# A triangle product in four channels at a time: three of four channels of the core with seventeen half-width products, in place of two of three

## The chip, the cores and the metric

The kernel runs on one core of a Trainium2 chip. The metric is the device time of one execution in microseconds (us). Before the change the median of three runs is 3130.55 us (3130.3 to 3131.14).

## The reference, cut to what matters

The input is x, 384 x 384 positions with 128 features. Two layers follow each other. The first holds the operation that this change is about:

```python
z = _layernorm(x, norm_g, norm_b)
left = (z @ Wl + bl) * jax.nn.sigmoid(z @ Wlg + blg)
right = (z @ Wr + br) * jax.nn.sigmoid(z @ Wrg + brg)
core = jnp.einsum('bikh,bjkh->bijh', left, right)
zo = _layernorm(core, onorm_g, onorm_b) @ Wout + bout
```

The einsum is, for each of the 128 channels h, a product of two 384 x 384 matrices. The core is then normalized over the channels, so the kernel also keeps for every position (i, j) the sum over the channels and the sum of squares. The second layer (a gated product with row sums) is not touched.

## The kernel before, in words

The kernel has three stages in time. The first normalizes x, makes left and right and writes them to a scratch tensor lr_d in HBM. The second is the core: channel by channel it loads left and right of the channel (the tile lrh, both interleaved), multiplies, and writes the result ct to core_d. The third reads core_d back and does everything else. Each wrapped instruction (`seq`) keeps its place in the program, so on every engine the order is the order of the code.

The change is in the second stage, in the loop over h at line 671. A channel's matrices are cut in blocks of 128 rows; N is 384 and J, half the width, 192. A product of one 128 x 128 block with 192 columns is called a half product here. There are two ways to do a channel:

- **Kind 0** (lines 675 to 695) is the plain way: nine products of 384 columns, eighteen half products, into three PSUM banks full3.
- **Kinds 1 and 2** (lines 696 to 747) compute the upper left 2 x 2 corner with seven products in place of eight, in the manner of Strassen and Winograd. They do three products of 384 columns into the bank b4 (third block row), and eleven half products into four banks b0 to b3: seventeen half products. GpSimd prepares sums of left blocks (`left_sums`, 613, four additions) and of right halves (`right_sums2`, 622, three subtractions) into small buffers, two sets of them (`sss`, `tts`). VectorE combines the banks: base and three terms (731 to 734), then `join` (661), which adds b0 and b1 to their terms and writes the first block row of ct, and `close` (665), which does this for b2 and b3, stores the channel and adds it to csum.

Before the change the kind is h % 3, for h from 0 to 125: 42 channels of each kind. The last two channels are done apart, plainly (754 on).

What stands in which place matters here. Everything that prepares channel h + 1 is issued inside channel h: `stay` (608, two copies of kept data on GpSimd), `left_sums`, `right_sums2` (if h + 1 is of kind 1 or 2), and `apart` (632), three ScalarE copies that take right out of the interleaved tile. The squares are made by `squares` on ScalarE (636) and added by `add_squares` on VectorE (639, 384 columns). At the end of a channel of kind 1 VectorE does one `add_squares` and then `join(h)` (743, 744); the next channel, of kind 2, starts with `close(h - 1)`. At the end of a channel of kind 2 VectorE does two `add_squares` (746, 747); `join` and `close` come only in the next channel, of kind 0, after its products were issued (679 to 681). All matmuls of these channels are issued by `product` at line 649; the VectorE additions out of PSUM by `add` at line 652.

A kind 0 channel uses the banks full3, so it does not touch b0 to b3, from which `join` and `close` still read. A channel of kind 1 or 2 starts with a product into b0 (699), then three into b4 (701), then b1, b2, b3 (728 to 730).

Loads of lrh (`load_h`, 85, called at 749) run three channels ahead, on SyncE's queue, as do the stores of ct.

Of the kernel before, what the change touches and what calls it, by code (L numbers as in the profile page):

```python
# [19 lines left out]
def triangle_then_gated_row_kernel(ctx: ExitStack, tc: tile.TileContext, a: dict, out: bass.AP):  # L20
# [17 lines left out]
    H = a["L0_side_b"].shape[0] // 4  # L38
# [17 lines left out]
    def seq(ins):  # L56

        return tc.keep_in_program_order(ins)
# [21 lines left out]
    with ExitStack() as ctx2:  # L80
# [481 lines left out]
        with tc.tile_pool(name="p2r", bufs=2, side="right", reuse_waits="tile") as rrp, \  # L562
# [9 lines left out]
            right = {}  # L572

            def fill(h):

                if h < H:
# [15 lines left out]
                    if h == 0:  # L592
                        stay()

            J = N // 2
            js = slice(0, J), slice(J, N)
            terms2 = arena[:, 2:4].rearrange("p b n -> p (b n)").rearrange("p (q j) -> p q j", j=J)
            base = arena[:, 6, js[0]]
            tts = [arena[:, n:n + 2].rearrange("p b n -> p (b n)").rearrange("p (q j) -> p q j", j=J) for n in (0, 4)]
            sss = [[arena[:, 2 * NB + 1, n * P:(n + 1) * P] for n in range(3)] + [arena[:, 6, J:J + P]],  # L600
                   [wz[:, n * P:(n + 1) * P] for n in range(4)]]
            sq = arena[:, NB:2 * NB]
            cts = {}
# [8 lines left out]

            def left_sums(h):

                ss = sss[h % 3 - 1]
                for n, x, y, op in ((0, block(h, 0, 1), block(h, 0, 0), ALU.subtract),
                                    (1, block(h, 0, 1), block(h, 1, 1), ALU.add),
                                    (2, ss[1], block(h, 0, 0), ALU.subtract),
                                    (3, block(h, 1, 0), ss[2], ALU.subtract)):
                    seq(nc.gpsimd.tensor_tensor(ss[n], x, y, op))  # L620

            def right_sums2(h):

                rr, tt = right[h], tts[h % 3 - 1]
                seq(nc.gpsimd.tensor_tensor(
                    tt[:, 0:2], rr[:, 0, js[1]].unsqueeze(1).to_broadcast([P, 2, J]),
                    rr.rearrange("p b n -> p (b n)").rearrange("p (a m) -> p a m", a=2)[:, :, js[0]], ALU.subtract,
                ))
                seq(nc.gpsimd.tensor_tensor(tt[:, 2], rr[:, 0, js[0]], tt[:, 1], ALU.subtract))
                seq(nc.gpsimd.tensor_tensor(tt[:, 3], rr[:, 1, js[0]], tt[:, 2], ALU.subtract))  # L630

            def apart(h, k):

                seq(nc.scalar.copy(right[h][:, k], loaded2[h][:, k, :, 1]))  # L634
# [4 lines left out]
            def add_squares(c, ib=slice(0, NB)):  # L639
                seq(nc.vector.tensor_add(csq[:, ib], c, csq[:, ib]))  # L640
# [14 lines left out]
            with tc.tile_pool(name="p2mix", bufs=1, space=PSUM, reuse_waits="tile") as mps:  # L655
                full3 = [mps.tile([P, 512], F32, name="r%d" % n)[:, :N] for n in range(NB)]
                half4 = [mps.tile([P, 512], F32, name="b%d" % n) for n in range(4)]
                b4 = mps.tile([P, 512], F32, name="b4")[:, :N]
                b0, b1, b2, b3 = (b[:, :J] for b in half4)

                def join(h):
                    for b, j, n in (b0, js[0], 0), (b1, js[1], 1):
                        add(cts[h][:, 0, j], b, terms2[:, n])

                def close(h):
                    for b, j, n in (b2, js[0], 2), (b3, js[1], 3):
                        add(cts[h][:, 1, j], b, terms2[:, n])
                    store_core(h)
                    add_sum(cts[h])

                for h in range(H - 2):
                    cts[h] = op.tile([P, NB, N], F32, tag="ct", name="ct")
                    right[h + 1] = rrp.tile([P, NB, N], F32, tag="rr", name="rr")
                    kind, rr, ct = h % 3, right[h], cts[h]
                    if kind == 0:
                        for i in range(NB):
                            for k in range(NB):
                                product(full3[i], block(h, k, i), rr[:, k], k == 0, k == NB - 1)
                        if h > 0:
                            join(h - 1)  # L680
                            close(h - 1)
                        stay(h + 1)
                        left_sums(h + 1)
                        for k in range(NB - 1):
                            apart(h + 1, k)
                        right_sums2(h + 1)
                        seq(nc.scalar.copy(ct[:, 0], full3[0]))
                        if h > 0:
                            for ib in range(NB):
                                squares(cts[h - 1][:, ib], half4[ib][:, :N])  # L690
                                add_squares(half4[ib][:, :N], ib)
                        apart(h + 1, NB - 1)
                        seq(nc.scalar.copy(ct[:, 1], full3[1]))
                        for ib in range(2):
                            add_sum(full3[ib], ib)
                    else:
                        ss, tt = sss[kind - 1], tts[kind - 1]
                        B = [[rr[:, k, j] for j in js] for k in range(NB)]
                        product(b0, block(h, 0, 0), B[0][0])
                        for k in range(NB):  # L700
                            product(b4, block(h, k, 2), rr[:, k], k == 0, k == NB - 1)
                        stay(h + 1)
                        if kind == 1:
                            seq(nc.scalar.copy(cts[h - 1][:, 2], full3[2]))
                            store_core(h - 1)
                            add_sum(full3[2], 2)
                            seq(nc.scalar.copy(terms2[:, 0], b0))
                            left_sums(h + 1)
                            for ib in range(2):
                                squares(full3[ib], full3[ib])  # L710
                                add_squares(full3[ib], ib)
                            for k in range(NB - 1):
                                apart(h + 1, k)
                            right_sums2(h + 1)
                            seq(nc.scalar.copy(ct[:, 2], b4))
                            squares(full3[2], full3[2])
                        else:
                            close(h - 1)
                            seq(nc.scalar.copy(terms2[:, 0], b0))
                            for ib in 0, 2:  # L720
                                squares(cts[h - 1][:, ib], full3[ib])
                            apart(h + 1, 0)
                            squares(cts[h - 1][:, 1], full3[1])
                            apart(h + 1, 1)
                            add_squares(full3[0], 0)
                            seq(nc.scalar.copy(ct[:, 2], b4))
                        apart(h + 1, NB - 1)
                        product(b1, ss[2], tt[:, 2])
                        product(b2, ss[1], tt[:, 0])
                        product(b3, ss[0], tt[:, 1])  # L730
                        add(base, b1, terms2[:, 0])
                        add(terms2[:, 2], b3, base)
                        add(terms2[:, 1], b2, base)
                        add(terms2[:, 3], b3, terms2[:, 1])
                        product(b0, block(h, 1, 0), B[1][0], True, False)
                        product(b0, block(h, 2, 0), B[2][0], False, True)
                        product(b1, ss[3], B[1][1], True, False)
                        product(b1, block(h, 2, 0), B[2][1], False, True)
                        product(b2, block(h, 1, 1), tt[:, 3], True, False)
                        product(b2, block(h, 2, 1), B[2][0], False, True)  # L740
                        product(b3, block(h, 2, 1), B[2][1])
                        if kind == 1:
                            add_squares(full3[2], 2)
                            join(h)
                        else:
                            for ib in 1, 2:
                                add_squares(full3[ib], ib)
                    del right[h], loaded2[h]
                    load_h(h + 3)
                join(h)  # L750
                close(h)
            with tc.tile_pool(name="p2ps", bufs=2, space=PSUM, reuse_waits="tile") as ps, \
                 tc.tile_pool(name="p2one", bufs=1, space=PSUM, reuse_waits="tile") as ps1:
                for h in range(H - 2, H):
                    t, rr = loaded2.pop(h), right.pop(h)
# [16 lines left out]
                    ct = op.tile([P, NB, N], F32, tag="ct", name="ct")  # L772
# [363 lines left out]
```

## Time and profile before

The profiled execution took 3133.74 us by its own time; its span from the first to the last instruction is 3131.9 us, so 1.8 us lie around it. It is 3.2 us (0.1%) above the median of the three runs.

| | first stage | core, h < 126 | last two channels | third stage |
|---|---|---|---|---|
| stretch of the span, us | 0 to 1011 | 1011 to 1719 | 1719 to 1740 | 1740 to 3132 |
| TensorE busy, us | 1005.6 | 706.9 | 20.2 | 1378.7 |
| VectorE busy, us | 833.7 | 566.7 | 13.7 | 1226.3 |
| ScalarE busy, us | 491.5 | 439.1 | 12.9 | 1014.3 |
| GpSimd busy, us | 813.9 | 450.7 | 5.8 | 1117.2 |
| share of the DMA engines | 0.77 | 0.98 | 0.94 | 0.61 |

How to read it and the lines below: PE is TensorE's matmul, PEld its weight load, DVE is VectorE, ACT ScalarE, POOL GpSimd, SP SyncE. Busy time counts only stretches in which an instruction of the engine was running; the end of a matmul is modelled, so consecutive matmuls overlap in the records, and the pace is read from their starts. A float32 matmul of the program is executed as two passes, and each pass is one record. A row of the timeline is: start, length, engine, line, operation, out<-in, shape, count, and in brackets the idle time of the engine before it and what ended it.

### The profile page before, as it was taken

How to read it: one execution, taken by the hardware profiler on the slowest of the kernel's cores; microseconds unless marked ns; L12 is line 12 of the kernel's file. 1: busy time of each engine (PE TensorE's matmuls, PEld its weight loads, DVE VectorE, ACT ScalarE, POOL GpSimd, SP SyncE). 2: the span in 40 equal slices, each digit the busy share in tenths (PEclk: the TensorE clock that was granted, in tenths of full speed). 3: DMA queues.
4: the chain of work that ended last, by engine and by line, in shares of the span. 5: the costliest groups of instructions: out<-in, count | busy, mean ns of one | idle time of the engine just before them, and what ended most of it. 6: DMA issues, size and time to landing. Idle time of an engine off the chain costs nothing.

```text
span 3131.9 us, 48235 instructions
## 1 busy us (share of the span) xinstructions
PE 3111.3 (99%) x12146; PEld 2234.8 (71%) x12146; DVE 2640.4 (84%) x8415; ACT 1957.8 (63%) x4551; POOL 2387.5 (76%) x3150
## 2 busy tenths in 40 slices
PE   9999999999999999999999999999999999999998
PEld 4677777777776777777777666777777777777776
DVE  8888888888886778877878788888888888888998
ACT  4444444444444666665665577777777777777776
POOL 6888888888886666666666588788887888888887
PEclk9999999999999999999999999999999999999999
DMA  4888878788783999999999866666666666666562
GB/s 154 330 310 295 336 273 332 288 320 314 289 336 91 283 293 293 293 294 292 293 294 294 281 217 224 217 221 217 221 222 222 222 222 215 222 218 221 204 217 107
DMA packets 509124, 797.66 MB, mean 255 GB/s; under 512 B 56689, under 2 KB 419569, under 8 KB 492466
## 3 DMA queue, kind: packets, MB, share of 16 engines
q1 hardware_dynamic: 507952, 793.20, 74.5%
q8 instruction: 101, 1.65, 0.2%
q14 instruction: 173, 1.42, 0.1%
q10 hardware_dynamic: 834, 1.18, 0.1%
q0 software_dynamic: 64, 0.20, 0.0%
HBM read 508.14 MB, written 286.36 MB: 254 GB/s over the span
## 4 chain that ended last, share of the span: by engine, by line
PE 98%; DVE 1%; issue 0%; POOL 0%; ACT 0%; DMA 0%; POOLq 0%; ACTq 0%; DVEq 0%; SPq 0%
PE pr L372 31%; PE b L649 15%; PE py L934 8%; PE pr L905 8%; PE pg L922 8%; PE pl L923 8%; PE r L649 8%; PE pg L874 8%; PE py L935 4%; DMA core_d<-ct 0%; PE pc L764 0%; POOL rs L286 0%; PE pq L882 0%; PE pt L335 0%; DVE lr L385 0%
## 5 line engine op out<-in xcount | busy, mean ns | idle before, releaser
L372 PE MATMUL pr<-wz,xc 128*128 128x512 f32 x2176 | 935.2, 592 | 1.4 <-POOL xc L324 1.4
L372 PEld LDWEIGHTS pr<-wz,xc 128*128 128x128 f32 x2176 | 670.5, 308 | 265.4 <-POOL xc L324 2.8
L383 ACT ACTIVATE sg<-pr,rs 128x256 f32<-128x256 f32 x1152 | 482.7, 470 | 510.9 <-ACT sg L383 355.4
L385 DVE SCALAR_TENSOR_TENSOR lr<-pr,rs,sg 128x256 f32<-128x256 f32 x1152 | 501.9, 477 | 165.5 <-ACT sg L383 160.1
L969 ACT ACTIVATE py<-py,nm,rs 128x128 f32<-128x128 f32 x1149 | 492.1, 429 | 158.4 <-DVE u L927 80.9
L934 PEld LDWEIGHTS py<-wo,u 128*128 128x128 f32 x2304 | 376.6, 191 | 97.5
L934 PE MATMUL py<-wo,u 128*128 128x128 f32 x2304 | 402.1, 275 | 0.0
L896 POOL TENSOR_TENSOR cs<-ct,rt 128x384 f32<-128x384 f32 x380 | 378.5, 997 | 10.2 <-DMA rt<-rstd_d 6.7
L1004 POOL TENSOR_TENSOR yt<-yt,lnb 128x384 f32<-128x384 f32 x380 | 379.6, 1000 | 2.9 <-DVE yt L998 2.6
L649 PE MATMUL b<-rr,lrh 128*128 128x192 f32 (+1 forms) x1512 | 374.4, 379 | 0.0
L324 POOL TENSOR_TENSOR xc<-xc,bc 128x512 f32<-128x512 f32 x272 | 345.7, 1271 | 24.0
L286 POOL TENSOR_TENSOR rs<-nd,mhalf 128x8 f32<-128x8 f32 (+1 forms) x145 | 236.2, 1629 | 147.0 <-ACT sg L383 107.4
L949 DVE BATCH_NORM_STATS2 st<-py 128x6 f32<-128x128 f32 x1152 | 266.5, 287 | 88.1 <-PE py L935 86.1
L905 PE MATMUL pr<-cs,wc 128*128 128x384 f32 x768 | 313.6, 490 | 1.4 <-DVE cs L894 1.4
L935 PE MATMUL py<-ident,x1T 128*128 128x128 f32 x1152 | 314.0, 273 | 0.0
L922 PE MATMUL pg<-x1T,mat_L_conv_W_gate 128*128 128x384 f32 x768 | 310.7, 486 | 0.9 <-ACT g L925 0.9
L874 PE MATMUL pg<-xt,mat_L_conv_Wg 128*128 128x384 f32 x768 | 310.7, 487 | 0.2 <-ACT ct L788 0.2
L923 PE MATMUL pl<-x1T,mat_L_conv_W_left 128*128 128x384 f32 x768 | 310.5, 486 | 0.0
L649 PEld LDWEIGHTS b<-rr,lrh 128*128 128x128 f32 x1512 | 268.4, 196 | 53.0
L634 ACT COPY rr<-lrh 128x384 f32<-128x384 f32 x378 | 204.7, 549 | 149.4 <-DMA lrh<-lr_d 89.8
L925 ACT ACTIVATE g<-pg,col_L_conv_b_gate 128x384 f32<-128x384 f32 x384 | 222.7, 580 | 104.2 <-PE pg L922 94.0
L876 ACT ACTIVATE gT<-pg,col_L_conv_bg 128x384 f32<-128x384 f32 x384 | 220.4, 576 | 105.0 <-PE pg L874 105.0
(167 smaller groups left out, 5272.7 us busy)
## 6 DMA issues: line engine op xcount, KB each, us to landing
lr_d<-lr SPq DMA_DIRECT2D x128, 1024.0 KB
lrh<-lr_d SPq DMA_DIRECT2D x128, 640.0 KB
xt<-in_x_row_dram SPq DMA_DIRECT2D x96, 768.0 KB
ct<-core_d SPq DMA_DIRECT2D x95, 768.0 KB
rt<-rstd_d SPq DMA_DIRECT2D x95, 768.0 KB
core_d<-ct SPq DMA_DIRECT2D x126, 576.0 KB
out_dram<-yt SPq DMA_DIRECT2D x94, 768.0 KB
xt<-in_x_nat_dram SPq DMA_DIRECT2D x136, 512.0 KB
```

What stands on the lines that cost most here:

```text
L372: seq(nc.tensor.matmul(pr[:, r, :], lhsT=columns[n][:, 4 * q + i, :] if n < PLAIN else columns[n][:, q, :, i], rhs=wz, start=True, stop=Tr ...
L383: seq(nc.scalar.activation(sg[r], pr[:, r, 2 * H:], AF.Sigmoid, scale=rs[r]))
L385: seq(nc.vector.scalar_tensor_tensor(t[:, :, c * XR + r0 + r, :], pr[:, r, :2 * H].rearrange("k (h s) -> k h s", s=2), rs[r], sg[r].rearra ...
L649: seq(nc.tensor.matmul(to, lhsT=lhsT, rhs=rhs, start=start, stop=stop))
L874: seq(nc.tensor.matmul(pg[:, :N], lhsT=wg0, rhs=r["xT"], start=True, stop=True))
L905: seq(nc.tensor.matmul(pr[:, :N], lhsT=wc, rhs=r["cs"], start=True, stop=True))
L922: seq(nc.tensor.matmul(pg2[:, :N], lhsT=wgate, rhs=r["x1T"], start=True, stop=True))
L923: seq(nc.tensor.matmul(pl[:, :N], lhsT=wleft, rhs=r["x1T"], start=True, stop=True))
L934: seq(nc.tensor.matmul(py[:, s], lhsT=r["u"][:, s], rhs=r["wo"], start=True, stop=False))
L935: seq(nc.tensor.matmul(py[:, s], lhsT=r["x1T"][:, s], rhs=ident, start=False, stop=True, is_transpose=True))
L969: seq(nc.scalar.activation(py[:, s], py[:, s], AF.Identity, bias=bias, scale=scale))
L1004: seq(engine.tensor_tensor(yt, yt, lnbb, ALU.add))
```

## The change

The list `kinds` takes the place of h % 3. The channels 0 to 5 stay 0, 1, 2, 0, 1, 2; from channel 6 on the pattern is 0, 1, 2, 3, thirty times; two entries 0 stand for the channels that are done apart. The name `last` says that the next channel is of kind 0. A channel of kind 3 takes the same branch of the code as kind 2, and the first of the two sets of buffers, as kind 1 does. A channel of kind 2 that is followed by kind 3 now also prepares the sums of h + 1 (`left_sums`, `right_sums2`) and does `join(h)` at its end, after its two `add_squares`. The line numbers of the changed kernel are two higher in the helpers (651 for the matmuls, 654 for the additions).

```diff
+            kinds = [0, 1, 2] * 2 + [0, 1, 2, 3] * ((H - 8) // 4) + [0, 0]
...
-                ss = sss[h % 3 - 1]
+                ss = sss[(kinds[h] - 1) % 2]
...
-                rr, tt = right[h], tts[h % 3 - 1]
+                rr, tt = right[h], tts[(kinds[h] - 1) % 2]
...
-                    kind, rr, ct = h % 3, right[h], cts[h]
+                    kind, rr, ct = kinds[h], right[h], cts[h]
+                    last = kinds[h + 1] == 0
...
-                        ss, tt = sss[kind - 1], tts[kind - 1]
+                        ss, tt = sss[(kind - 1) % 2], tts[(kind - 1) % 2]
...
                             close(h - 1)
                             seq(nc.scalar.copy(terms2[:, 0], b0))
+                            if not last:
+                                left_sums(h + 1)
                             for ib in 0, 2:
                                 squares(cts[h - 1][:, ib], full3[ib])
                             apart(h + 1, 0)
                             squares(cts[h - 1][:, 1], full3[1])
                             apart(h + 1, 1)
+                            if not last:
+                                right_sums2(h + 1)
                             add_squares(full3[0], 0)
...
-                        if kind == 1:
-                            add_squares(full3[2], 2)
+                        for ib in (2,) if kind == 1 else (1, 2):
+                            add_squares(full3[ib], ib)
+                        if not last:
                             join(h)
-                        else:
-                            for ib in 1, 2:
-                                add_squares(full3[ib], ib)
```

More of the change, by code (lines that the diff above doesn't have):

```diff
@@ L593, in fill @@
                         stay()
+            kinds = [0, 1, 2] * 2 + [0, 1, 2, 3] * ((H - 8) // 4) + [0, 0]
+            assert len(kinds) == H
             J = N // 2
```

## The prediction

> **What bounds the kernel now.** I read the page first (busy shares, granted clock), then the busy time of four consecutive channels of the core, then the chain of waits, the waits of that stage, and last the timeline around the ends of two channels.
>
> ```profile
> PE 3111.3 (99%) x12146; PEld 2234.8 (71%) x12146; DVE 2640.4 (84%) x8415; ACT 1957.8 (63%) x4551; POOL 2387.5 (76%) x3150
> ...
> PEclk9999999999999999999999999999999999999999
> ```
>
> TensorE is busy 99% of the span at full granted clock. A busy PE may still be a PE with modelled ends, so the stage itself has to be looked at. These are the channels of kind 0, 1, 2 and again 0 around 1300 us; the columns are PE, PEld, DVE, ACT, POOL with counts, granted clock, share of the DMA engines and GB/s (the first row starts inside its channel):
>
> ```profile
> 1299.31:1304.27 4.96, 4.96 (x17) 2.95 (x16) 3.52 (x7) 2.98 (x7) 3.07 (x6) 1.00 0.99 302
> 1304.27:1309.78 5.51, 5.51 (x30) 4.75 (x29) 4.31 (x12) 3.68 (x9) 4.46 (x10) 1.00 0.96 289
> 1309.78:1315.29 5.51, 5.51 (x30) 4.75 (x30) 4.87 (x11) 3.27 (x8) 2.66 (x5) 1.00 1.02 297
> 1315.29:1321.09 5.80, 5.80 (x19) 3.53 (x19) 4.37 (x10) 3.54 (x8) 3.60 (x7) 1.00 0.94 281
> ```
>
> A channel of kind 0 takes 5.80 us of PE, one of kind 1 or 2 takes 5.51; no engine but PE fills its channel, and VectorE comes nearest (4.87 of 5.51). The DMA engines are as good as always busy, which I come back to. The chain shows the same without a gap, and repeats it in every triple of the stage:
>
> ```profile
> 1299.91 4.51 PE r L649 x14
> 1304.43 11.02 PE b L649 x56
> 1315.45 4.84 PE r L649 x15
> ```
>
> Two channels with banks b take 11.02 us; a whole piece "r" of 18 passes takes 5.80 (5.805 from its starts). Asked for the waits between 1020 and 1719 us, PE and PEld answer with no row at all. VectorE has these:
>
> ```profile
> DVE arena L652 <- PE b L649: 55.7, 167, 0.4
> DVE csq L640 <- ACT b L637: 53.7, 41, 2.2
> ```
>
> So PE sets the pace of this stage, and VectorE waits for PE inside each channel of kind 1 and 2 (167 times, two per channel). This matters below: what VectorE does after such a wait keeps a fixed distance from PE.
>
> **What the change takes away.** Channels of kind 0 in the loop go from 42 to 32 (2 + 30), the others from 84 to 94. Ten channels go from 5.805 to 5.510 us: 10 x 0.295 = 2.95 us less, all of it on the path, if PE keeps running without a gap. That is the whole gain to be had: 0.09% of the kernel.
>
> **What it adds beside the path.** Each of the ten channels adds seven GpSimd operations; in the groups by form the four left sums take 0.57 + 0.57 + 0.46 + 0.46 and the three right sums 1.00 + 0.59 + 0.65, together 4.3 us, so 43 us on an engine that is busy 451 of the stage's 708. I cost them at nothing: in channels of kind 1 the same seven fit behind the loads. For kind 3 they are made in kind 2, where GpSimd idles (2.66 of 5.51 us busy); the copies there end 1 to 3 us into the channel, the sums would need about 4.3 more, and the first product that reads them starts 2.26 us into the next channel, 7.8 us after the start. The cover is 0.5 us or more; if it is gone, PE waits for GpSimd by what is over. ScalarE issues nothing more per channel than in kind 2 now. The DMAs stay the same in number and place in their queue.
>
> **What it adds on the path: a hand-over.** Here the order of VectorE decides. The built program shows that the first product of kind 3, into b0, waits for the `join` addition that reads b0 of the kind 2 channel ahead of it. In kind 1 the same wait exists, ahead of kind 2. But kind 1 does one `add_squares` before `join`, and kind 2 does two. First the end of a kind 1 channel, then the end of a kind 2 channel:
>
> ```profile
> 1309.10 0.61 DVE L652 TENSOR_TENSOR ct<-b,arena 128x192 f32<-128x192 f32 x2
> ...
> 1309.61 0.36 PEld L649 LDWEIGHTS b<-rr,lrh 128*128 128x128 f32 x2
> ```
>
> ```profile
> 1314.61 0.55 DVE L640 TENSOR_TENSOR csq<-r,csq 128x384 f32<-128x384 f32 x1
> ...
> 1315.07 0.35 DVE L652 TENSOR_TENSOR ct<-b,arena 128x192 f32<-128x192 f32 x1
> 1315.12 0.36 PEld L649 LDWEIGHTS r<-rr,lrh 128*128 128x128 f32 x2
> 1315.29 0.49 PE L649 MATMUL r<-rr,lrh 128*128 128x384 f32 x1
> ```
>
> In the first, the read of b0 starts at 1309.10 and ends at 1309.45, and the weights of the next channel's b0 are loaded at 1309.61: 0.16 us early, no wait. In the second it ends at 1315.07 + 0.35 = 1315.42, while the next channel starts at 1315.29: 0.13 us late. Today that harms nobody, since kind 0 writes other banks. In the changed kernel that place holds the first product of kind 3, and in all 42 channels of kind 2 the distance is the same within 1 ns, because VectorE waited for PE just before.
>
> To the 0.13 comes the hand-over itself: the trace of before has no wait of this kind in this stage, so I bound it from two places in the third stage, where PE stood waiting for VectorE:
>
> ```profile
> 1736.30 0.56 DVE L560 SCALAR_TENSOR_TENSOR arena<-arena 128x384 f32<-128x384 f32 x1
> ...
> 1737.01 0.56 PE L893 MATMUL pb<-arena,ident 128*128 128x384 f32 x1 [0.43 <-DVE arena L560]
> ```
>
> ```profile
> 1740.64 1.02 DVE L894 TENSOR_TENSOR cs<-ct,pb 128x384 f32<-128x384 f32 x2 [3.77 <-DMA ct<-core_d]
> ...
> 1741.24 0.59 PE L905 MATMUL pr<-cs,wc 128*128 128x384 f32 x1 [1.42 <-DVE cs L894]
> ```
>
> At L893 the producer ends at 1736.86 and the matmul starts 0.15 later; it is 0.07 longer than the usual 0.49 of this shape, as the weights come first: 0.22 in all. At L905 the first of the two additions ends at 1741.19 (0.55 each), the matmul starts 0.05 later and is 0.10 longer: 0.15. The wait at L893 is an instruction of its own ahead of the matmul, at L905 it is the matmul's. Kind 3's b0 also has a wait of its own, but that one stands already in PE's sequencer when the addition ends, as the wait at 1309 does. I take the middle, 0.19. Below zero it can't be: nothing of this hand-over exists now.
>
> So PE stands 0.13 + 0.19 = 0.32 us at the start of each kind 3 (bounds 0.28 and 0.35). Everything on PE is queued behind it: the weight load and the whole channel. VectorE does not wait for it; its `close` and csum run on.
>
> **Is there a second wait behind it?** In kind 2, `join` to the first csq takes from 1309.10 to 1312.28 (3.18), and base is ready to be added 2.79 us after the channel's start. In kind 3 `join` starts 0.22 before the old start of the channel, so 0.54 before the delayed one: VectorE is ready at 2.64 and still waits for PE. Spare are 0.15 us, and about 0.26 more before a bank is written late. So the delay is paid once per group and doesn't grow.
>
> Here a rule speaks against the change. The Trainium skill, "SBUF — State Buffer", section "SBUF: two separate sides", says that VectorE's operations with two SBUF inputs and GpSimd's share one port pair, and that whoever starts first holds it for the whole instruction. The csum addition (L643, 1152 columns) is such an operation, and GpSimd now has sums to make in kind 2 that may reach into kind 3's csum. By the rule it could be held for a GpSimd operation of 1.00 us, 0.6 beyond the spare time: 30 x 0.6 = 18 us. By the rows of before csum takes 1.36 to 1.80 us, mean 1.40, though GpSimd runs beside it in kind 2: at most 0.44 more, 0.03 beyond the spare time. I take the row: nothing. The upper end of the range keeps some of it.
>
> **The sum.** Per group of four channels: 5.805 + 3 x 5.510 + 0.32 = 22.655 us; thirty groups 679.65, the two triples at the front 2 x 16.825 = 33.65, together 713.3. Before it was 42 x 16.825 = 706.65. Difference +6.65 (30 x 0.32 = 9.6 less 2.95), with the bounds of the hand-over +5.45 to +7.55. The profiled execution of 3133.74 us would become 3140.4 (span 3138.6); it stands 3.2 above the median, and the same difference on 3130.55 gives 3137.2 us.
>
> **The rivals.**
> - *The gain is realized whole* (the other side). `join` is early enough after all, for instance because PE takes the dependency at a later pass: 3130.55 - 2.95 = 3127.6. For it: PE never waited in this stage. Against: the last of its covers is short by 0.13 us even with a hand-over of zero. It decides at a `join` 0.3 us earlier. Chance 0.08.
> - *The delay grows.* VectorE falls behind in three such channels in a row, by the port or by GpSimd's sums being late for kind 3's b1: another 0.1 to 0.6 us per group, 3140 to 3155, most likely near 3143. For it: VectorE has the least spare time (4.87 of 5.51). Against: the spare time above, and that base waits for PE in every kind 2. Chance 0.15.
> - *The transfers bound it.* With the DMA share at 0.98, a faster PE would find loads late, and the stage would stay at its 706.65: 3130.5. Against: the delayed group runs at 5.66 us per channel, slower than 5.61 now, so loads get more time, not less. This can decide only if the hand-over costs nothing. Chance 0.05.
> - The change does what it says: the built program has ten more such channels and 70 more GpSimd rows.
>
> **How the numbers follow.** The forecast has 0.72. Its own range is 3136.0 to 3138.1. To hold 8 in 10 the range takes a little of an underrated hand-over below and the nearer part of the growing delay above: 3134.8 to 3141. A difference of 0.2%, 6.3 us, is about what a measurement of this kernel can tell from no change; the forecast is just above it. Two thirds of the forecast and all of the growing delay lie above (0.63 together); the rest of the forecast, the transfers and most of the whole gain, which is under 0.2%, count as no change (0.33); 0.04 for a gain by something I don't see.
>
> **What would show it.** Right: about thirty waits of PE or PEld at L651 for DVE's ct at L654, none shorter than 0.1 us, at one distance of 22.65 us, and no other wait of PE in the stage; kind 2 channels of 5.83 us where 3 follows, others unchanged; granted clock still 1.00. Wrong: no such wait (then 3127.6); waits for POOL arena or for DVE arena at b1 to b3 (then the delay grows); a stage of more than 716 us, or a wait of more than 0.4 us each.

## The result and the profile after

The changed kernel takes 3138.3 us (median of 11 runs) against 3130.7 for the kernel before (11 runs): ratio 1.0022, 95% interval 1.0014 to 1.003, that is 4.4 to 9.4 us more. 3137.2 was forecast. The 3138.3 lies inside the stated range (3134.8 to 3141) and just above the forecast's own (3136.0 to 3138.1).

The span of the profiled execution rose from 3131.9 to 3135.0 us only, while the core stage alone (first product of channel 0 to the first of the two plain channels at the end) rose from 708.0 to 714.5. The difference lies where no line differs: in this execution the first stage was 1.8 us shorter, and what follows the core stage 1.6 us. So stages are compared below, and times only by their medians.

The chain of waits of the changed kernel, around the same place:

```profile
1293.61 5.80 PE r L651 x18
1299.41 11.02 PE b L651 x56
1310.43 0.07 issue
1310.50 5.76 PE b L651 x28
1316.26 5.80 PE r L651 x18
```

Kind 1 and 2 still take 11.02 us together and kind 0 still 5.80. What is new is between kind 2 and kind 3: a gap that was not there before, 0.07 us of it shown as a gap and the rest as a longer piece, 5.76 where 5.51 were to come. The weight load, which waited for nothing in this stage before, has one row of waits now:

```profile
PEld b L651 <- issue: 9.9, 30, 0.3
```

Thirty waits, one per group of four. The profile names "issue" as the releaser and not VectorE, because the semaphore is waited for in an instruction of its own ahead of the weight load. Who it is, the timeline shows:

```profile
1309.94 0.96 PE L651 MATMUL b<-rr,lrh 128*128 128x192 f32 x3
1310.05 0.87 DVE L654 TENSOR_TENSOR ct<-b,arena 128x192 f32<-128x192 f32 x3
1310.47 0.31 PEld L651 LDWEIGHTS b<-rr,lrh 128*128 128x128 f32 x2 [0.33 <-issue]
```

`join`'s read of b0 begins at 1310.05 and takes 0.35, to 1310.40; 0.07 later the weights of kind 3's first product are loaded, after 0.33 us without a weight load. From the starts of the matmuls, kind 2 and kind 3 together take 11.335 us where two such channels took 11.020: 0.315 us per group, 30 x 0.315 = 9.5, less 2.95 gives the 6.5 of the stage.

### The profile page after: what moved, and what is told of

Same layout as the page of the kernel before. It is cut to its first block, busy times and chain, and to the rows that moved or that the text cites. A ratio compares the mean times of both kernels' runs of the same rounds, so it can differ in the third digit from the quotient of the medians.

```text
span 3135.0 us, 48765 instructions
## 1 busy us (share of the span) xinstructions
PE 3115.4 (99%) x12246; PEld 2246.9 (72%) x12246; DVE 2663.7 (85%) x8475; ACT 1951.9 (62%) x4541; POOL 2440.6 (78%) x3220
## 4 chain that ended last, share of the span: by engine, by line
PE 98%; DVE 1%; ACT 0%; issue 0%; POOL 0%; POOLq 0%; ACTq 0%; DVEq 0%
PE pr L372 31%; PE b L651 17%; PE py L939 8%; PE pr L910 8%; PE pg L927 8%; PE pl L928 8%; PE pg L879 8%; PE r L651 6%; PE py L940 4%; PE pc L769 0%; PE pq L887 0%; PE pt L335 0%; POOL rs L286 0%; ACT py L974 0%; DVE st L263 0%
## 5 line engine op out<-in xcount | busy, mean ns | idle before, releaser
L651 PE MATMUL b<-rr,lrh 128*128 128x192 f32 x1692 | 423.9, 381 | 2.1
L651 PEld LDWEIGHTS b<-rr,lrh 128*128 128x128 f32 x1692 | 298.9, 196 | 65.5 <-issue 9.9
```

The source lines that it names most:

```text
L651: seq(nc.tensor.matmul(to, lhsT=lhsT, rhs=rhs, start=start, stop=stop))
```

## The experiments

Times are medians; the differences are against the kernel before in the same session of runs. "Stage" is the core stage of the profiled execution.

**Join first.** In kind 2, ahead of kind 3:

```diff
+                        if kind == 2 and not last:
+                            join(h)
                         for ib in (2,) if kind == 1 else (1, 2):
                             add_squares(full3[ib], ib)
-                        if not last:
+                        if kind == 1:
                             join(h)
```

> The changed kernel, but a channel of kind 2 that is followed by kind 3 does join ahead of its two add_squares. Theory (PE waits only because b0 is read 0.93 us too late, behind two squares): the read of b0 ends 0.8 us before the next channel starts, the thirty waits of 0.315 us go away, the core stage falls from 714.5 to 705.05 us, and the kernel is 2.95 us faster than before the change (ratio 0.9991). Rival (three such channels in a row are too much for VectorE or for GpSimd, wherever join stands): the wait moves to b1, b2 or the sums, and the stage stays above 708.

Measured: stage 705.6 us (one stray wait of 0.4), 3128.0 against 3131.1 us, ratio 0.999 (0.9981 to 0.9998). The chain:

```profile
1290.78 5.80 PE r L651 x18
1296.58 16.53 PE b L651 x84
1313.11 5.80 PE r L651 x18
```

Three channels in one piece of 16.53 = 3 x 5.51. The wait was the place of `join` and nothing else; the work is the same.

**Join between the two squares**, with one ahead of it as in kind 1:

> The changed kernel, but in kind 2 join stands between the two add_squares, so that one stands ahead of it, as in kind 1. Theory: the read of b0 ends about 0.33 us before the next channel's first matmul, as it does in kind 1, and no wait is left: stage 705.05 us, same time as with join first. If the hand-over needs more than 0.33 us, a small wait stays (stage between 705 and 708). Rival (load of VectorE): as in the changed kernel, stage near 714.

Measured: stage 705.1, 3128.0 us, ratio 0.9991 (0.9983 to 0.9999). As expected: 0.33 us of lead is enough.

**Join later**, behind all three squares of the channel:

```diff
-                            add_squares(full3[0], 0)
+                            if last:
+                                add_squares(full3[0], 0)
...
-                        for ib in (2,) if kind == 1 else (1, 2):
+                        for ib in (2,) if kind == 1 else (1, 2) if last else (0, 1, 2):
```

> The changed kernel, but all three add_squares of a kind 2 channel that is followed by kind 3 stand ahead of join (the first is taken from the middle of the channel). Same work, join 0.46 us later. Theory: each of the thirty waits grows by 0.46 us to 0.78, the stage to 714.5 + 13.9 = 728.4 us, the kernel to about 20 us above before. Rival (the loss is the amount of work, not the place of join): stage unchanged at 714.5.

Measured: stage 728.4, 3152.4 us, ratio 1.0068 (1.0055 to 1.008). The same work in another order costs 14 us. The chain at one group:

```profile
1315.41 0.53 issue
1315.94 5.76 PE b L651 x28
```

The gap of 0.07 us has become 0.53, and the longer piece is the same: 0.78 us per group. `join` is 0.465 us later, from the ends of its reads, and the group is 0.465 us longer, from the starts of the matmuls.

**b4 first.** The other end of the dependency is moved: kind 3 does its three b4 products ahead of the one into b0.

```diff
-                        product(b0, block(h, 0, 0), B[0][0])
+                        if kind < 3:
+                            product(b0, block(h, 0, 0), B[0][0])
                         for k in range(NB):
                             product(b4, block(h, k, 2), rr[:, k], k == 0, k == NB - 1)
+                        if kind == 3:
+                            product(b0, block(h, 0, 0), B[0][0])
```

> The changed kernel with its late join, but a channel of kind 3 begins with the three products into b4 and does its first product into b0 after them, 1.94 us later. Theory (what PE waits for is bank b0 alone, still to be read by join): the read of b0 is done 1.8 us before its bank is written, no wait is left, stage 705 us, kernel 3 us faster than before the change. Rival (any start of a third such channel is late, by load): a wait of about 0.3 us stays, stage near 714.

A miss. Measured: stage 721.2, 3145.4 us, ratio 1.0044 (1.003 to 1.0058). The wait at the start of kind 3 is gone (kind 2 takes 5.51), but kind 3 takes 6.02, with a wait at b1's second product. ScalarE and VectorE in such a channel:

```profile
1364.91 0.32 ACT L725 COPY arena<-b 128x192 f32<-128x192 f32 x1 [4.20 <-PE b L651]
1365.12 0.91 ACT L639 ACTIVATE r<-ct 128x384 f32<-128x384 f32 x2
```

```profile
1365.65 0.56 DVE L642 TENSOR_TENSOR csq<-r,csq 128x384 f32<-128x384 f32 x1 [0.69 <-ACT r L639]
1366.13 0.81 DVE L654 TENSOR_TENSOR arena<-b,arena 128x192 f32<-128x192 f32 x2
```

ScalarE's copy of b0 waits for the late product; the squares stand behind it in ScalarE's queue, VectorE's csq waits for the squares, and base stands behind csq. To test this chain, the copy was moved behind the two squares and a copy of right:

> The run with b4 first, but in kind 3 ScalarE's copy of b0 into its term stands behind two of the squares and one of the copies of right, no longer ahead of them. Theory (with b4 first the wait for join was gone, and what took its place was only that the squares stood behind this copy in ScalarE's queue, VectorE's csq behind the squares, and base behind csq): no wait is left, stage 705 us, kernel 3 us faster than before the change. Rival (there is another reason why a late b0 costs 0.5 us): stage near 721.

Measured: kind 3 takes 5.51 again, in 29 of 30 channels. The stage is 707.2 and not 705, mainly by one wait of PE of 1.6 us at one place, which begins with a load:

```profile
1094.25 0.55 ACT L636 COPY rr<-lrh 128x384 f32<-128x384 f32 x1 [4.16 <-DMA lrh<-lr_d]
1097.65 1.49 DVE L642 TENSOR_TENSOR csq<-b,csq 128x384 f32<-128x384 f32 x3 [4.56 <-ACT b L639]
1098.26 0.92 PE L651 MATMUL b<-rr,lrh 128*128 128x192 f32 x3 [1.59 <-DVE csq L642]
```

ScalarE waits for a late lrh, the squares stand behind that copy in its queue, VectorE's csq waits for the squares, and the next channel's b0 for csq. Why this load was late is open. The times: 3130.4 against 3132.3 us, ratio 0.9994 (0.9985 to 1.0003): the half microsecond per group is gone, the gain of 3 us is not shown by the times.

**No plain channel.** Join first in kinds 2 and 3, and kinds 1, 2, 3, 2, 3 and so on after channel 0:

```diff
-            kinds = [0, 1, 2] * 2 + [0, 1, 2, 3] * ((H - 8) // 4) + [0, 0]
+            kinds = [0, 1] + [2, 3] * ((H - 4) // 2) + [0, 0]
```

> Only channel 0 is of kind 0; all others of the loop are 1, 2, 3, 2, 3 and so on, and each of kind 2 or 3 does join ahead of its two add_squares. Theory (PE sets the pace as long as join is early): 5.51 us a channel, stage 7.2 + 125 x 5.51 = 695.9 us, 12.1 us faster than before the change. Rival 1 (transfers): at a DMA share of 0.98 with 5.61 us a channel they cannot follow 5.51, PE waits for lrh and the stage stays above 700. Rival 2 (GpSimd: 0.6 to 1.7 us of copies and 4.3 us of sums in every channel of 5.51): PE waits for the sums at b1, stage above 708.

Measured: stage 736.9, 3159.7 us, ratio 1.0091 (1.0077 to 1.0105). GpSimd is the bound (rival 2): busy 284 of 300 us, and the weight load waits for its sums:

```profile
PEld b L651 <- POOL arena L631: 51.7, 39, 1.3
```

From three of these channels, a subtraction of GpSimd and VectorE's csum beside it:

```profile
1302.58 1.59 POOL L632 TENSOR_TENSOR arena<-rr,arena 128x192 f32<-128x192 f32 x1
1307.72 0.59 POOL L631 TENSOR_TENSOR arena<-rr,arena 128x192 f32<-128x192 f32 x1
1313.53 1.75 POOL L631 TENSOR_TENSOR arena<-rr,arena 128x192 f32<-128x192 f32 x1
```

```profile
1302.24 1.47 DVE L645 TENSOR_TENSOR csum<-ct,csum 128x1152 f32<-128x1152 f32 x1
1307.75 1.77 DVE L645 TENSOR_TENSOR csum<-ct,csum 128x1152 f32<-128x1152 f32 x1
1313.47 1.36 DVE L645 TENSOR_TENSOR csum<-ct,csum 128x1152 f32<-128x1152 f32 x1
```

Alone, either subtraction takes 0.59 us. At 1302.58 it starts after csum, is 1.00 longer and ends 0.46 after csum has ended (1303.71). At 1307.72 GpSimd starts first, and csum takes 1.77 in place of 1.36. That is the rule that the prediction weighed (The Trainium skill, "SBUF — State Buffer", "SBUF: two separate sides"), in both directions. At 1313.53 it is L631 that is held, and b1's first product waits for it. L631 is stretched in 39 of the 125 channels, and in just these 39 PE waits for it.

**Without csum**, in the same pattern; the addition is left out for channels 1 to 124:

> The pattern without plain channels, but the addition of ct to csum is left out for channels 1 to 124, so the mean over the channels is not the reference's. Theory (csum's 1152 columns with two SBUF inputs shut GpSimd out for about 1 us per channel, and so GpSimd was the bound at 5.84 us): GpSimd needs 4.85 us per channel, PE sets the pace again, stage 695.9 us. Rival (the transfers cannot follow 5.51 us per channel): the stage stays above 700, and PE waits for lrh. VectorE has 1.4 us less to do per channel as well, which this run does not tell apart from the port.

Measured: stage 695.9, as worked out; 3119.8 us, ratio 0.9963 (0.9948 to 0.9977). PE waits for nothing in the core's loop, at a DMA share of 1.01: the transfers can follow 5.51 us a channel, so rival 1 falls. GpSimd is busy 247 of 300 us, VectorE 217, and no GpSimd subtraction is stretched. The row has the busy times of PE, PEld, DVE, ACT and POOL, granted clock, DMA share and GB/s:

```profile
1100.00:1400.00 300.00, 300.00 (x1524) 258.11 (x1523) 216.76 (x600) 180.60 (x436) 246.82 (x492) 1.00 1.01 299
```

VectorE has less to do here as well; the run with csum's third row from PSUM, below, tells the two apart.

**Fewer plain channels**, with join first:

> Join first, and one plain channel in five (0, 1, 2, 3, 2; the last group has six). Stage 7.16 + 24 x 5.805 + 101 x 5.51 = 703.0 us, 5.0 us faster than before the change, if GpSimd recovers in each plain channel what it lost in four (4 x 0.33 = 1.3 us, where the spare time is 2.5 us mostly). If it does not, PE waits for the sums and the stage lies above 703.

> Join first, and one plain channel in six (0, 1, 2, 3, 2, 3). If GpSimd holds the pace with one plain channel in six (it needs 5.84 us for a channel with sums where PE gives 5.51, by the run without plain channels, so it falls 0.33 us behind in each; the spare time at the first product that reads its sums is 2.5 us mostly, and 1.0 at worst), the stage is 7.16 + 20 x 5.805 + 105 x 5.51 = 701.8 us and the kernel 6.2 us faster than before the change. If five in a row are too many, PE waits for the sums in the last of them, by up to 0.6 us in each of 21 groups: stage up to 714.

Measured: four of five, stage 703.3 and 3127.8 us, ratio 0.9988 (0.9981 to 0.9994); five of six, stage 703.9 and 3129.0 us, ratio 0.9992 (0.9984 to 1.0001), with waits for the sums in its trace (the longest 1.3 us). One more channel in the row brought nothing here: GpSimd's spare time is used up. The times fell by less than the stages; whether other executions have more such waits is open.

**csum's third row from PSUM.** Nothing is left out; b4 still holds the row when `join` is done:

```diff
-                    add_sum(cts[h])
+                    add_sum(cts[h][:, :2], slice(0, 2))
...
+                        if not last:
+                            join(h)
+                        add_sum(b4, 2)
                         for ib in (2,) if kind == 1 else (1, 2):
                             add_squares(full3[ib], ib)
-                        if not last:
-                            join(h)
```

> No plain channel after the first, join first, and the third block row of csum is added from bank b4 in PSUM (384 columns, one SBUF input) right after join, so that the addition with two SBUF inputs shrinks from 1152 to 768 columns; nothing is left out. Theory (GpSimd was the bound because csum shuts it out): its time per channel falls by about 0.4 us, from 5.84 to 5.44, under PE's 5.51; PE sets the pace, stage 695.9 us, kernel 12.1 us faster than before the change. Rival (VectorE was near its limit as well: it gains one more instruction, about 0.1 us, and would need 5.3 to 5.6 us per channel): PE waits for VectorE's base or terms, stage above 700.

> The same way of adding csum with one plain channel in six. Theory: GpSimd keeps its spare time through five channels, the waits for the sums that the run with one plain channel in six had are gone, stage 701.8 us, 6.2 us faster than before the change. If VectorE is the bound in a row of five, waits for VectorE take their place and the stage stays at 704 or more.

Measured: without plain channels, stage 700.1 and 3122.9 against 3131.3 us, ratio 0.9971 (0.996 to 0.9983): the fastest of the kernels that leave nothing out. PE's waits for the right sums are gone, and these are back at 1.00 and twice 0.59. GpSimd still shows 283 of 300 us busy, as csum now mostly meets one of the two copies of `stay` (in the mean a copy takes 0.655 us, 0.290 with csum as it was), and PE does not wait for these. VectorE does thirteen operations a channel in place of twelve, so it was the held GpSimd, and not VectorE's load, that cost the time before.

The stage stops short of 695.9: channels take 5.535 in the median and VectorE is busy 97% of the time, so the rival is right as well. From the starts of the matmuls, most of the lost 0.025 us lies at the first b4 product. In 94 channels csum's read of b4 ends less than 0.16 us ahead of it, and some 0.02 us is lost there in the median; in the other 30 of kinds 2 and 3 it ends earlier, and nothing is. It looks like the last read of a bank again, but no run here moves it.

With one plain channel in six: stage 702.4, 3126.0 us, ratio 0.9983 (0.9976 to 0.999), and no wait for sums in its trace. The same kind of row for the pattern without plain channels, with csum as it was, and then with the row from PSUM:

```profile
1100.00:1400.00 300.00, 288.53 (x1442) 242.49 (x1441) 273.15 (x618) 173.56 (x409) 283.85 (x463) 1.00 0.94 280
```

```profile
1100.00:1400.00 300.00, 299.88 (x1519) 255.91 (x1517) 290.10 (x705) 181.82 (x432) 282.98 (x488) 1.00 1.00 297
```

## Why the prediction was right, point by point

- *What bounds the stage, and the gain.* Right. The ten channels were worth 2.95 us; the two kernels with an earlier join got 3.1 us in time.
- *The hand-over.* Right in mechanism and size: 0.315 us measured per group, 0.32 forecast. Of it 0.13 is the lateness of `join`; the hand-over itself is 0.18, where 0.19 was taken between 0.15 and 0.22. Join first and join between take the whole wait away, and join later adds to it just what `join` is later. Two details differ: the profile calls the wait "issue", and the longer channel shows as 5.74 for kind 2 and 5.59 for kind 3, not 5.83 for kind 2.
- *The sum.* Stage +6.53, forecast +6.65. (The forecast's 706.65 and 713.3 leave out that the first channel takes 7.16 us; that is so in both kernels.) The median rose by 7.6; its interval holds both, and the runs can't tell whether the last microsecond is real. The profiled execution's own time was forecast at 3140.4 and is 3136.8: adding a difference to one execution's time takes its chance with it, here 3.4 us in stages that no edit touches.
- *GpSimd's additions cost nothing.* Right here: PE never waits for the sums, and the spare time at the first product that reads them was 1.8 us at least. The bound given, 0.5, was too careful. But there was no room for many more: without plain channels GpSimd became the bound.
- *The delay does not grow.* Right: every wait is 0.3 us. csum took 1.43 us in the mean (1.40 before) and 1.74 at most, so the row of before was the better guide to its size. The rule on the shared port cost nothing in this change: csum is held by up to 0.4 us and GpSimd's operations by up to 1.2, and both had that time to spare. It decided the pattern without plain channels.
- *The rivals.* The whole gain came only when join was moved ahead by 0.46 us or more. The transfers do not bound the stage, though their share is 0.98: without csum they served 5.51 us a channel. One late load did cost PE 1.6 us, in the trace of b4 first with the copy later.

## What to carry to other kernels

When an optimized step is to follow another of its kind, look for the last read of its buffers ahead of it: a read that was harmless in front of a different step can become a wait on the critical engine, and 0.3 us thirty times is more than three times what ten cheaper steps brought here. The cure is an order, not less work: put what frees a buffer ahead of what nobody waits for. When the late product is moved instead, follow every queue behind it; here the wait came back through ScalarE's and VectorE's queues.

## What the runs showed of the hardware

A DMA share of 0.98 to 1.01 did not bound the stage: the same engines moved 291 GB/s in it before, and 299 without csum, with no wait for them on PE. A hand-over from VectorE to a waiting TensorE cost 0.18 us from the end of the addition to the point from which the matmuls run at full pace, 0.07 of it until the weight load starts. And a GpSimd subtraction of 0.59 us was stretched to 1.59 by a VectorE addition with two SBUF inputs that had started before it; where the subtraction had started first, the addition took 1.77 us in place of 1.36.
